# A decoder layer on one core: dense products issued whole or as four 32-column strips, score fills in 32x64 tiles

## The chip, the core and the metric

The kernel runs on one core of one Trainium2 chip. A core has five engines that run their own instruction streams and wait for each other at semaphores: TensorE (PE, matrix products; its weight loads are listed apart as PEld), VectorE (DVE), ScalarE (ACT), GpSimd (POOL) and SyncE (SP, which here issues DMA). Matrix products read SBUF and write PSUM, which has eight banks of 2 KB for each of 128 partitions.

TensorE's array has 128 rows (the contraction) and 128 columns (the outputs). It can be used whole, or divided into tiles that work side by side: 128 rows by 32 columns gives four tiles ("strips"), 32x128 gives four, 32x64 eight, 64x32 eight. The tile that a product uses follows from the partitions of its operands and of its output.

The metric is the device time of one execution in microseconds (us), the median of the runs.

## What is computed

One decoder layer over x of 16 batches x 512 tokens x 256 channels: a gated long convolution with an MLP, then causal self-attention and cross-attention with 16 heads of 16 channels, then a low-rank FFN, each with a residual and a layernorm.

```python
z = rmsnorm(u, pre_w) @ in_w.T                 # three projections, a 3-tap convolution, a long convolution
y = (yconv + xv * D_skip) * x2 ; y = y @ out_w.T + u
zm = rmsnorm(y, post_w)
x = layernorm(x + y + gelu(zm @ l1.T) * (zm @ l2.T) @ l3.T)      # l1, l2: 256 -> 672
...
q, k, v = heads(x @ Wq + bq), heads(x @ Wk + bk), heads(x @ Wv + bv)
y = softmax(mask(q k^T / 4)) v + softmax(qc kc^T / 4) vc         # 512 own keys, 64 cross keys
x = layernorm(x + y @ Wp + bp)
...
P = x @ U1 ; H = gelu(P @ V1 + b1) ; Q = H @ U2                  # 256 -> 64 -> 1024 -> 64 -> 256
x = layernorm(x + Q @ V2 + b2)
```

## The kernel before

Everything is float32, and each product then takes two passes through the array (two weight loads and two matmul records in the trace); a transposition takes one. The kernel has two stages. The first (to about 300 us) does the projections and the long convolution for all batches. The second goes through the 16 batches: `first_block` (gate, output projection, MLP), `attention` and `ffn`.

No engine's order is written by hand. Each piece of work is handed to `Plan.op` (line 78) with the engines that can run it, an estimated cost, a priority and the buffers that it holds; `Plan.schedule` (line 103) plays the program through with those costs, always takes the startable piece with the best rank, and `emit` issues the result. The instructions of every engine are thus in a fixed order, which overlaps three batches: batch b's attention runs beside the MLP of b+1 and the FFN of b-1. A piece on PE names its tiling; `change` (line 95) adds to its rank: staying in a divided shape is favoured by `STAY` (1000), and a piece that isn't urgent is held back by `HOLD` (1000) when it would leave the whole shape. `EMPTY` is the planner's allowance for a change of shape.

What runs on PE in the second stage, with the tile shape that each uses before:

- dense products, whole (128x128): `to_tokens` L1083, `outp` L1148, the MLP's L1187 and L1239, values L1268, context keys L1292 and values L1317, queries and keys L1340, the FFN's ends L1761 and L1807;
- transpositions, whole: L348, L1359, L1507;
- score fills, 32x128: `maxima` L1435 (12 per batch) and the exponentials' fills in `sums` L1557 (10 per batch), four heads side by side; the cross-attention's L1615 (2 per batch) in 32x64;
- weighted sums L1587 and the MLP's remainder L1217, strips (128x32); the cross sums L1635, 64x32;
- the FFN's middle: L1778 (64x128, two tiles) and L1794 (128x64, two tiles).

All score fills, of `maxima`, of `sums` and of the cross-attention, write one buffer: the pool `scores` has a single tile of four banks. A fill of `maxima` is read by DVE (a mask, L1484, and two or three maxima, L1486 to L1497); in batches 0, 1, 13, 14 and 15 ACT copies it out instead (L1458). A fill of `sums` or of the cross-attention is read by ACT's exponential (L1527). The next fill of any kind waits until that reader is done. In batches 0, 1 and 15 the fills are cut in two halves. The other products share three banks (`mm`) and one accumulator bank (`av`).

```python
"scores": tiles(psum, "scores", 1, [P, HPG, T]),
"av": tiles(psum, "av", 1, [P, T]),
"mm": tiles(psum, "mm", 3, [P, T]),
```

## Time and profile before

| | |
|---|---|
| time, median of 3 runs | 2083.39 us (2082.22 to 2087.12) |
| the profiled execution, its span | 2082.0 us |
| matmul records on PE | 14900 |
| granted TensorE clock, mean | 0.992 |
| DVE, ACT, POOL busy | 1331.5, 1029.1, 768.5 us |

The profile is of one execution. In its list of groups, a line is a line of the kernel, `out<-in` names the tiles, `128*32 128x512` is a matmul with 128 contraction rows and 32 output columns that streams 512 columns. Matmuls are pipelined: the length of one record holds the way through the array, so that what a product costs is read from start to start.

### The profile page before, as it was taken

The page shows a single profiled execution, that of the slowest core. Times are in us where ns is not written, and L with a number is a line of the kernel's source. Part 1 is how long each engine was busy: PE and PEld are TensorE (multiplying, and loading weights), DVE is VectorE, ACT ScalarE, POOL GpSimd, SP SyncE. Part 2 cuts the span into 40 slices and gives each one's busy share as a digit, 9 for nine tenths or more (in the row PEclk, how much of TensorE's full clock was granted, in tenths as well). Part 3 has the DMA queues.
Part 4 walks back from the last instruction along what each step waited for, and adds up shares of the span by engine and source line. Part 5 has one row for each costly group of instructions (what it writes and reads, how often), then busy time and mean ns, then how long its engine had stood idle before and what let it go on. Part 6 is the DMA issues. An engine that isn't in the chain of part 4 may idle for free. (4 is left out here: it accounts for less than half of the span.)

```text
span 2082.0 us, 36834 instructions
## 1 busy us (share of the span) xinstructions
PE 2005.5 (96%) x14900; PEld 1054.2 (51%) x14900; DVE 1331.5 (64%) x1922; ACT 1029.1 (49%) x1463; POOL 768.5 (37%) x1036
## 2 busy tenths in 40 slices
PE   8999978999999999999999999999999999999987
PEld 4455645555554545454545454454545454545443
DVE  7987543736584848484857576666767584656554
ACT  7863422656435262717161626253534446655773
POOL 7694622243323241414142424232323233533432
PEclk9999989999999999999999999999999999999999
DMA  5365861040304040313131312222131404031200
GB/s 200 109 211 179 269 221 51 6 119 17 119 11 144 12 134 22 123 33 118 37 108 48 100 56 88 68 71 85 58 98 33 123 13 129 17 101 44 72 22 31
DMA packets 114939, 182.22 MB, mean 88 GB/s; under 512 B 13393, under 2 KB 62034, under 8 KB 114642
## 3 DMA queue, kind: packets, MB, share of 16 engines
q1 hardware_dynamic: 113234, 177.26, 27.6%
q8 instruction: 117, 1.92, 0.4%
q10 hardware_dynamic: 1536, 2.62, 0.4%
q14 instruction: 52, 0.43, 0.1%
HBM read 111.09 MB, written 68.76 MB: 86 GB/s over the span
## 5 line engine op out<-in xcount | busy, mean ns | idle before, releaser
L1527 ACT ACTIVATE ex<-scores 128x2048 f32<-128x2048 f32 (+1 forms) x228 | 362.5, 1606 | 193.4 <-PE scores L1557 140.8
L1187 PE MATMUL mm<-xT,w_l 128*128 128x512 f32 x640 | 299.5, 608 | 0.0
L1574 POOL TENSOR_SCALAR_AFFINE_SELECT ex<-ex 128x512 f32<-128x512 f32 x256 | 159.1, 637 | 324.5 <-ACT ex L1527 323.1
L1435 PE MATMUL scores<-keys,q 32*128 32x192 f32 (+5 forms) x2848 | 225.3, 426 | 6.2 <-ACT ex L1458 4.6
L1557 PE MATMUL scores<-q,keys 32*128 32x256 f32 (+3 forms) x2240 | 183.3, 435 | 11.8 <-ACT ex L1527 10.9
L1435 PEld LDWEIGHTS scores<-keys,q 32*128 32x128 f32 x2848 | 123.8, 184 | 138.5 <-issue 41.1
L1786 ACT ACTIVATE row<-mm,b_s 128x512 f32<-128x512 f32 x124 | 79.0, 687 | 224.6 <-PE mm L1778 223.9
L1187 PEld LDWEIGHTS mm<-xT,w_l 128*128 128x128 f32 x640 | 114.5, 190 | 141.4 <-issue 133.9
L1717 POOL TENSOR_TENSOR nd<-nd,nd 128x1024 f32<-128x1024 f32 x30 | 70.8, 2358 | 299.2 <-DMA nd<-di 299.2
L1587 PE MATMUL av<-ex,va 128*32 128x512 f32 (+3 forms) x2048 | 164.8, 438 | 0.9 <-POOL ex L1574 0.9
L1239 PE MATMUL mm<-w_l,gT 128*128 128x256 f32 x640 | 160.6, 386 | 0.0
L308 POOL TENSOR_SCALAR small<-small 128x4 f32<-128x4 f32 (+1 forms) x66 | 13.3, 201 | 393.7 <-DVE small L1047 358.8
L500 DVE SCALAR_TENSOR_TENSOR frow<-fmm,cw,frow 128x511 f32<-128x511 f32 x192 | 141.1, 744 | 25.9 <-ACT frow L492 21.2
L1484 DVE TENSOR_TENSOR scores<-scores,mask_qk 128x1024 f32<-128x1024 f32 x132 | 115.6, 876 | 60.9 <-PE scores L1435 57.8
L1557 PEld LDWEIGHTS scores<-q,keys 32*128 32x128 f32 x2240 | 96.9, 184 | 107.5 <-ACT ex L1527 67.0
L1199 ACT ACTIVATE row<-mm 128x512 f32<-128x512 f32 x80 | 47.8, 598 | 209.4 <-PE mm L1187 209.4
L1458 ACT COPY ex<-scores 128x1024 f32<-128x1024 f32 (+1 forms) x96 | 114.4, 1228 | 65.6 <-PE scores L1435 52.9
L485 PE MATMUL fmm<-fx,inw 128*128 128x512 f32 x312 | 143.4, 604 | 0.0
L1239 PEld LDWEIGHTS mm<-w_l,gT 128*128 128x128 f32 x640 | 117.2, 190 | 44.6 <-issue 31.1
L299 DVE COPY row<-av 128x512 f32<-128x512 f32 x60 | 41.5, 692 | 134.9 <-PE av L1587 124.5
L1340 PE MATMUL mm<-xT,wqc_s 128*128 128x512 f32 x256 | 126.3, 611 | 0.0
L1346 DVE TENSOR_SCALAR q<-mm,bqc_s 128x512 f32<-128x512 f32 x62 | 46.5, 750 | 100.4 <-PE mm L1340 100.3
(212 smaller groups left out, 3489.3 us busy)
## 6 DMA issues: line engine op xcount, KB each, us to landing
dn<-row SPq DMA_DIRECT2D x120, 256.0 KB
keys<-dk SPq DMA_DIRECT2D x64, 256.0 KB
nd<-dn SPq DMA_DIRECT2D x30, 512.0 KB
nd<-di SPq DMA_DIRECT2D x30, 512.0 KB
fx<-hpad SPq DMA_DIRECT2D x28, 512.0 KB
early<-gates SPq DMA_DIRECT2D x16, 512.0 KB
early<-yconv SPq DMA_DIRECT2D x32, 256.0 KB
dk<-row SPq DMA_DIRECT2D x32, 256.0 KB
```

Of the source, the lines that this page charges most:

```text
L485: nc.tensor.matmul(ps.t, inw[:, k, bass.ts(m, P)], xT.t[:, k, :], start=(k == 0), stop=(k == KD - 1))
L500: lambda e, lag=lag: nc.vector.scalar_tensor_tensor(t.t[:, lag:], ps.t[:, 0 : T - lag], cw[:, m, 2 - lag : 3 - lag], t.t[:, lag:], ALU.mul ...
L1187: nc.tensor.matmul(ps.t, w[:, k, bass.ts(f, P)], zT.t[:, k, :], start=(k == 0), stop=(k == KD - 1))
L1239: nc.tensor.matmul(ps.t[:, bass.ts(cc, D)], gT.t[:, f, bass.ts(c, P)] if f < NF else gE.t, w_l3[:, f, :] if f < NF else w_l3e[:, c, :], st ...
L1340: nc.tensor.matmul(ps.t, w[:, k, cols], xT.t[:, k, :], start=(k == 0), stop=(k == KD - 1))
L1435: nc.tensor.matmul(sc.t[:, r, lo:hi], q.t[hd, bass.ts(i, P)], kk.t[hd, k0 - at + lo : k0 - at + hi], start=True, stop=True,)
L1458: lambda e, sc=sc, both=both, cols=cols: nc.scalar.copy(both.t[:, :, cols], sc.t[:, :, cols]),
L1484: nc.vector.tensor_tensor(diag, diag, mask, ALU.add)
L1527: lambda e: nc.scalar.activation(ex.t.rearrange("p (r n) -> p r n", r=HPG)[:, :, cols], sc.t[:, :, cols], AF.Exp, scale=scale),
L1557: nc.tensor.matmul(sc.t[:, r, lo:hi], keys[g].t[hd, TC + j * P : TC + (j + 1) * P], qas[g].t[hd, q0 + lo : q0 + hi], start=True, stop=True,)
L1574: lambda e, ex=ex, at=at: nc.gpsimd.affine_select(out=ex.t.rearrange("p (r n) -> p r n", r=HPG)[:, :, at : at + P], in_=ex.t.rearrange("p ...
L1587: nc.tensor.matmul(av[g].t[bass.ts(r, SLOT), j * P :], va.t[:, j, h * VS : h * VS + SLOT], ex.t[:, r * T + at : r * T + at + n], start=(j ...
```

## The change

Products whose shape fits both get `flex=True`: the planner issues them whole when the array is whole, and otherwise as four products of 32 output columns each (`Plan.matmul`), so that they can follow the weighted sums, or one another, without a change of shape. Whole and strips are now both "plain" shapes, in which staying isn't favoured. All score fills use 32x64 (two products of 64 columns for each head), the FFN's L1778 uses 64x32 and its L1794 strips. The planner's allowances for a change of shape get other values, and are looked up by the shape entered instead of the one left. As the planner's costs and ranks change, the order on every engine changes too; the amount of work on DVE, ACT, POOL and SP is the same but for ten copies that go to DVE instead of ACT.

```diff
+STRIPS = (P, SLOT)
...
-    EMPTY = {P: 0.215, P // 2: 0.16, P // 4: 0.145}
+    EMPTY = {P: 0.2, P // 2: 0.148, P // 4: 0.121}
...
     def change(self, o, tiling):
-        if o.tiling == tiling:
-            return -self.STAY if tiling != FULL else 0
+        want, plain = self.mode(o, tiling), (FULL, STRIPS) if self.strips else (FULL,)
+        if want == tiling:
+            return -self.STAY if tiling not in plain else 0
         if o.urgent or o.tiling == FULL:
             return 0
-        return self.HOLD if tiling == FULL else -self.STAY / 2
+        return self.HOLD if tiling in plain else -self.STAY / 2
+
+    def mode(self, o, tiling):
+        return (tiling if tiling in (FULL, STRIPS) else STRIPS) if o.flex else o.tiling
+
+    def matmul(self, out, weights, moving, **kw):
+        rows, cols = self.now
+        n = weights.shape[-1]
+        for c in range(0, n, cols):
+            cs = slice(c, min(c + cols, n))
+            self.nc.tensor.matmul(out[cs], weights[:, cs], moving, **kw)
...
-                    o.empty = self.EMPTY[tiling[1]]
-                    tiling = o.tiling
+                    o.used = self.mode(o, tiling)
+                    if o.used != tiling:
+                        o.empty = self.EMPTY[o.used[1]]
+                    tiling = o.used
...
-    ROWS4, ROWS2, COLS4, COLS2, BOTH = (SLOT, P), (P // 2, P), (P, SLOT), (P, P // 2), (P // 2, SLOT)
+    COLS2, ROWS, BOTH = (P, P // 2), (SLOT, P // 2), (P // 2, SLOT)
...
-    plan = Plan(pool, 1000, 1000)
+    plan = Plan(pool, 1000, 1000, nc)
...
-                    gelus_pe[b].append(plan.op("PE", pe(T), mm, p1 - k, r=[(zT, k)], w=[ps]))
+                    gelus_pe[b].append(plan.op("PE", pe(T), mm, p1 - k, r=[(zT, k)], w=[ps], flex=True))
...
-                        "PE", cost_pe / len(cuts), mm, ps_, r=[q, kk], w=[(sc, h)], tiling=ROWS4, urgent=True
+                        "PE", cost_pe / len(cuts), mm, ps_, r=[q, kk], w=[(sc, h)], tiling=ROWS, urgent=True
...
             def hm(e, fp=fp, bank=bank):
-                for s in range(2):
-                    half = bass.ts(s, RANK)
-                    nc.tensor.matmul(bank(s), v1_s[half, bass.ts(fp, P)], pT.t[half, :], start=True, stop=True)
+                for c in range(0, P, SLOT):
+                    for s in range(2):
+                        half, at = bass.ts(s, RANK), fp * P + c
+                        plan.matmul(bank(s)[c : c + SLOT], v1_s[half, at : at + SLOT], pT.t[half, :], start=True, stop=True)
-            gelus_pe[window].append(plan.op("PE", tiled(T), hm, p3, r=[pT], w=hp, tiling=ROWS2))
+            gelus_pe[window].append(plan.op("PE", tiled(T), hm, p3, r=[pT], w=hp, tiling=BOTH))
...
-            plan.op("PE", tiled(T), qm, p3 - 1, r=hT, w=[acc], tiling=COLS2)
+            plan.op("PE", tiled(T), qm, p3 - 1, r=hT, w=[acc], tiling=STRIPS)
```

The other dense products get `plan.matmul` and `flex=True` in the same way. The first stage's plan is made without `nc`, so nothing in it is issued in strips; its order moves a little with the allowances.

More of the change, by code (lines that the diff above doesn't have):

```diff
@@ L58, in __init__ @@
         self.ready, self.start, self.end, self.engine = 0.0, None, None, None
-        self.tiling, self.urgent = FULL, False
+        self.tiling, self.urgent, self.flex, self.used = FULL, False, False, FULL
 class Plan:
@@ L70, with __init__, op @@
     CROSS = 0.18
-    def __init__(self, tiles, hold=0, stay=0):
+    def __init__(self, tiles, hold=0, stay=0, nc=None):
         self.tiles, self.ops = tiles, []
         self.HOLD, self.STAY = hold, stay
-    EMPTY = {P: 0.215, P // 2: 0.16, P // 4: 0.145}
-    def op(self, engines, cost, fn, prio, r=(), w=(), lat=0.0, after=(), tiling=FULL, urgent=False, holds=()):
+        self.nc, self.strips, self.now = nc, nc is not None, FULL
+    EMPTY = {P: 0.2, P // 2: 0.148, P // 4: 0.121}
+    def op(
+        self, engines, cost, fn, prio, r=(), w=(), lat=0.0, after=(), tiling=FULL, urgent=False, holds=(), flex=False
+    ):
         o = Op(len(self.ops), engines.split(), cost, lat, prio, fn)
-        o.tiling, o.urgent = tiling, urgent
+        o.tiling, o.urgent, o.flex = tiling, urgent, flex
         self.ops.append(o)
@@ L162, in schedule @@
                 o.engine, o.start = e, now
-                if e == "PE" and o.tiling != tiling:
-                    o.empty = self.EMPTY[tiling[1]]
-                    tiling = o.tiling
-                else:
-                    o.empty = 0.0
+                o.empty = 0.0
+                if e == "PE":
+                    o.used = self.mode(o, tiling)
+                    if o.used != tiling:
+                        o.empty = self.EMPTY[o.used[1]]
+                    tiling = o.used
                 until[e] = now + o.empty + (o.cost[o.engines.index(e)] if isinstance(o.cost, tuple) else o.cost)
@@ L193, in emit @@
                 b.t = self.tiles[b.cls][b.slot[1]]
+            self.now = o.used
             o.fn(o.engine)
@@ L698, in near_mm @@
                         )
-            plan.op("PE", 1.0, near_mm, pc - 60, r=[XV[kh], NEAR], w=[ps], tiling=COLS4, holds=[st])
+            plan.op("PE", 1.0, near_mm, pc - 60, r=[XV[kh], NEAR], w=[ps], tiling=STRIPS, holds=[st])
             def evac_state(e, ps=ps, st=st, blk=blk):
@@ L760, in far_mm @@
                             )
-            far_done = plan.op("PE", 1.0, far_mm, pc + 10, r=[st, far], w=ys, tiling=(SLOT, P // 2))
+            far_done = plan.op("PE", 1.0, far_mm, pc + 10, r=[st, far], w=ys, tiling=ROWS)
             for c in range(HPG):
@@ L1082, in mm @@
                     def mm(e, cp=cp, cc=cc, k=k, ps=ps):
-                        nc.tensor.matmul(
+                        plan.matmul(
                             ps.t[:, bass.ts(cc, D)], xT.t[:, k, bass.ts(2 * cp + cc, P)], w[:, k, :],
@@ L1086, in mm @@
                         )
-                    plan.op("PE", pe(D), mm, prio, r=[xT], w=[ps])
+                    plan.op("PE", pe(D), mm, prio, r=[xT], w=[ps], flex=True)
             add_op(ps, res, res, cp, prio)
@@ L1147, in outp @@
                     def outp(e, cp=cp, cc=cc, k=k, ps=ps):
-                        nc.tensor.matmul(
+                        plan.matmul(
                             ps.t[:, bass.ts(cc, D)], yt.t[:, k, bass.ts(2 * cp + cc, P)], outw[:, k, :],
@@ L1151, in outp @@
                         )
-                    plan.op("PE", pe(D), outp, p0, r=[(yt, k)], w=[ps], after=after)
+                    plan.op("PE", pe(D), outp, p0, r=[(yt, k)], w=[ps], after=after, flex=True)
             add_op(ps, x_, y1, cp, p0)
@@ L1186, in mm @@
                     def mm(e, f=f, w=w, k=k, ps=ps):
-                        nc.tensor.matmul(
+                        plan.matmul(
                             ps.t, w[:, k, bass.ts(f, P)], zT.t[:, k, :], start=(k == 0), stop=(k == KD - 1)
                         )
-                    gelus_pe[b].append(plan.op("PE", pe(T), mm, p1 - k, r=[(zT, k)], w=[ps]))
+                    gelus_pe[b].append(plan.op("PE", pe(T), mm, p1 - k, r=[(zT, k)], w=[ps], flex=True))
                     if f == HOLD:
@@ L1216, in mm_e @@
                     for c in range(NT):
-                        nc.tensor.matmul(
+                        plan.matmul(
                             ps.t[bass.ts(c, FE), bass.ts(n, P)], w[:, k, NF * P :], zT.t[:, k, bass.ts(c, P)],
@@ L1220, in mm_e @@
                         )
-        gelus_pe[b].append(plan.op("PE", 0.88, mm_e, p1, r=[zT], w=[ps], tiling=COLS4))
+        gelus_pe[b].append(plan.op("PE", 0.88, mm_e, p1, r=[zT], w=[ps], tiling=STRIPS))
         gelus[b].append(plan.op(
@@ L1238, in mm @@
                     def mm(e, c=2 * cp + cc, cc=cc, f=f, ps=ps):
-                        nc.tensor.matmul(
+                        plan.matmul(
                             ps.t[:, bass.ts(cc, D)],
@@ L1244, in mm @@
                         )
-                    plan.op("PE", pe(D), mm, p2, r=[(gT, f) if f < NF else gE], w=[ps])
+                    plan.op("PE", pe(D), mm, p2, r=[(gT, f) if f < NF else gE], w=[ps], flex=True)
             add_op(ps, x_, x_, cp, p2)
@@ L1267, in mm @@
                     def mm(e, jp=jp, jj=jj, k=k, ps=ps):
-                        nc.tensor.matmul(
+                        plan.matmul(
                             ps.t[:, bass.ts(jj, D)], xT.t[:, k, bass.ts(2 * jp + jj, P)], wv_s[:, k, :],
@@ L1271, in mm @@
                         )
-                    plan.op("PE", pe(D), mm, p0 + 40, r=[(xT, k)], w=[ps])
+                    plan.op("PE", pe(D), mm, p0 + 40, r=[(xT, k)], w=[ps], flex=True)
             plan.op(
@@ L1291, in kc_mm @@
                 for g in range(G):
-                    nc.tensor.matmul(
+                    plan.matmul(
                         ps.t[:, bass.ts(g, 2 * TC)], wck_s[:, bass.ts(g, P)], ctxT[:, b * TC : (b + 2) * TC],
@@ L1295, in kc_mm @@
                     )
-            plan.op("PE", 0.9, kc_mm, p0, w=[ps], after=begun)
+            plan.op("PE", 0.9, kc_mm, p0, w=[ps], after=begun, flex=True)
             plan.op(
@@ L1316, in attention @@
             "PE", pe(D),
-            lambda e, ps=ps: nc.tensor.matmul(
+            lambda e, ps=ps: plan.matmul(
                 ps.t[:, 0:D], twice.t.rearrange("c s t -> c (s t)"), wcv_s, start=True, stop=True
             ),
-            p0 + 45, r=[twice], w=[ps],
+            p0 + 45, r=[twice], w=[ps], flex=True,
         )
@@ L1339, in mm @@
                 def mm(e, k=k):
-                    nc.tensor.matmul(ps.t, w[:, k, cols], xT.t[:, k, :], start=(k == 0), stop=(k == KD - 1))
-                plan.op("PE", pe(T), mm, prio - k, r=[(xT, k)], w=[ps], holds=[dst])
+                    plan.matmul(ps.t, w[:, k, cols], xT.t[:, k, :], start=(k == 0), stop=(k == KD - 1))
+                plan.op("PE", pe(T), mm, prio - k, r=[(xT, k)], w=[ps], holds=[dst], flex=True)
             def ev(e):
@@ L1434, in mm @@
                                 hd = bass.ts(r, SLOT)
-                                nc.tensor.matmul(
+                                plan.matmul(
                                     sc.t[:, r, lo:hi], q.t[hd, bass.ts(i, P)], kk.t[hd, k0 - at + lo : k0 - at + hi],
@@ L1556, in mm @@
                                 hd, q0 = bass.ts(r, SLOT), j * P - at
-                                nc.tensor.matmul(
+                                plan.matmul(
                                     sc.t[:, r, lo:hi], keys[g].t[hd, TC + j * P : TC + (j + 1) * P],
@@ L1564, in sums @@
                         "PE", sum(tiled((T - j * P) // len(parts)) for _, j in uses), mm, p1 + 13,
-                        r=[x for kq in kqs.values() for x in kq], w=[(sc, h)], tiling=ROWS4, urgent=True,
+                        r=[x for kq in kqs.values() for x in kq], w=[(sc, h)], tiling=ROWS, urgent=True,
                     ))
@@ L1586, in wm @@
                             h = g * HPG + r
-                            nc.tensor.matmul(
+                            plan.matmul(
                                 av[g].t[bass.ts(r, SLOT), j * P :], va.t[:, j, h * VS : h * VS + SLOT],
@@ L1598, in sums @@
                         cost, wm, weights = wms.pop((g, j))
-                        plan.op("PE", cost, wm, pb_ - 6, r=[va, *weights], w=[av[g]], tiling=COLS4)
+                        plan.op("PE", cost, wm, pb_ - 6, r=[va, *weights], w=[av[g]], tiling=STRIPS)
                         left[g] = left[g][1:]
@@ L1614, in cm @@
                         for n in range(2):
-                            nc.tensor.matmul(
+                            plan.matmul(
                                 sc.t[bass.ts(n, TC), r, cols], kcs.t[hd, b % 2, g + n, :], cqas[g + n].t[hd, cols],
@@ L1621, in cross_scores @@
                     "PE", tiled(T // len(parts)) + 0.05, cm, p1 + 13, r=[kcs, cqas[g], cqas[g + 1]], w=[(sc, h)],
-                    tiling=(SLOT, P // 2), urgent=True,
+                    tiling=ROWS, urgent=True,
                 ))
@@ L1634, in cwm @@
                         part = bass.ts(half, TC)
-                        nc.tensor.matmul(
+                        plan.matmul(
                             cavs[half].t[bass.ts(r, SLOT), :], vc.t[part, g * HPG // 2 + r, :],
@@ L1760, in pt @@
             def pt(e, k=k, ps=ps):
-                nc.tensor.matmul(ps.t, u1_s[:, k, :], x2T.t[:, k, :], start=(k == 0), stop=(k == KD - 1))
-            plan.op("PE", pe(T), pt, p3 - k, r=[(x2T, k)], w=[ps])
+                plan.matmul(ps.t, u1_s[:, k, :], x2T.t[:, k, :], start=(k == 0), stop=(k == KD - 1))
+            plan.op("PE", pe(T), pt, p3 - k, r=[(x2T, k)], w=[ps], flex=True)
         plan.op("ACT DVE", (act(T), dve(T)), lambda e, ps=ps: copy(e, pT.t, ps.t), p3, r=[ps], w=[pT])
@@ L1793, in qm @@
                 for s in range(2):
-                    nc.tensor.matmul(
+                    plan.matmul(
                         acc.t[bass.ts(s, RANK), :], u2_s[:, 2 * fp + s, :], hT[s].t,
@@ L1806, in om @@
                 for cc in range(2):
-                    nc.tensor.matmul(
+                    plan.matmul(
                         ps.t[:, bass.ts(cc, D)], qT.t[:, bass.ts(2 * cp + cc, P)], v2_s, start=True, stop=True
                     )
-            plan.op("PE", 2 * pe(D), om, p4, r=[qT], w=[ps])
+            plan.op("PE", 2 * pe(D), om, p4, r=[qT], w=[ps], flex=True)
             add_op(ps, x_, x_, cp, p4)
```

## The prediction

> **What bounds the kernel now.** The page first: who is busy, and where in the span.

> ```profile
> span 2082.0 us, 36834 instructions
> PE 2005.5 (96%) x14900; PEld 1054.2 (51%) x14900; DVE 1331.5 (64%) x1922; ACT 1029.1 (49%) x1463; POOL 768.5 (37%) x1036
> ...
> PE   8999978999999999999999999999999999999987
> ```

> Then the same in a stretch of the steady batches, and PE's waits from 500 to 1700 us:

> ```profile
> 800.00:900.00 100.00, 99.67 (x712) 50.65 (x709) 64.86 (x93) 46.40 (x60) 31.76 (x44) 1.00 0.24 76
> ```
> ```profile
> PE scores L1557 <- ACT ex L1527: 3.0, 9, 0.3
> PE scores L1435 <- DVE maxes L1495: 1.1, 1, 1.1
> PE mm L348 <- ACT row L1786: 0.2, 1, 0.2
> ```

> PE is busy 99.67 of 100 us at full clock, and waits 4.3 us in 1200. So PE sets the time: what is taken from PE counts in full, and so does every wait that PE gets in exchange. The last view is the order of time around two changes of shape and around one fill of the maxima:

> ```profile
> 1199.55 1.50 PE L1587 MATMUL av<-ex,va 128*32 128x512 f32 x16
> 1200.98 1.13 PE L1268 MATMUL mm<-wv_s,xT 128*128 128x256 f32 x4
> 1202.04 1.11 PE L1615 MATMUL scores<-q,kcs 32*64 32x512 f32 x16
> 1203.08 1.08 PE L1217 MATMUL mm<-xT,w_l 128*32 128x128 f32 x32
> 1203.32 1.88 ACT L1527 ACTIVATE ex<-scores 128x2048 f32<-128x2048 f32 x1 [1.67 <-PE scores L1615]
> ...
> 1207.31 1.15 PE L1435 MATMUL scores<-keys,q 32*128 32x320 f32 x16
> 1208.53 1.23 DVE L1484 TENSOR_TENSOR scores<-scores,mask_qk 128x1024 f32<-128x1024 f32 x1 [0.49 <-PE scores L1435]
> 1209.80 0.69 DVE L1486 TENSOR_REDUCE maxes<-scores 128x8 f32<-128x512 f32 x1
> 1210.40 1.22 DVE L1489 TENSOR_REDUCE maxes<-scores 128x4 f32<-128x1024 f32 x1
> 1211.54 0.68 DVE L1492 TENSOR_REDUCE maxes<-scores 128x4 f32<-128x512 f32 x1
> ```

> How it is read: inside one shape, the trace's matmul starts follow each other by 0.429 us (512 columns), 0.216 (256) and 0.109 (128), however many tiles work side by side. The four passes of L1268 should take 0.863, but from its start to the next line's start is 1.06: 0.197 is the change of shape. It has two parts, the first weight load, which nothing covers (0.104 for 128 columns, 0.051 for 64, 0.024 for 32), and the emptying of the shape left (0.09 to 0.14). The fill L1435 has streamed its last column at 1208.28, DVE starts 0.25 later and is done at 1212.22, 3.69 after its start. The fill L1615, with eight tiles, has streamed at 1202.95 and ACT starts 0.37 later.

> **The change part by part.**

> **Strips instead of whole products: 0.** The order of the built programs has 28,218 matmuls instead of 14,900, but the passes, counted as groups that run side by side, are the same in both, and sum to 1756 us. The row L1217 shows strips at the pace of whole products: 32 matmuls of 128 columns are eight groups at 0.109, the four of a group starting within 0.02. The cover of the added instructions is the pass itself; without it, four starts of 0.0066 each would add 0.02 a pass.

> [...]

> **Changes of shape: -44.4 us.** Counted in the two orders, priced by the median of the same change in the trace. Before, 1082: into whole 386 x 0.213, into 32x128 353 x 0.198, strips 141 x 0.139, 128x64 80 x 0.153, 64x128 50 x 0.207, 32x64 40 x 0.145, 64x32 32 x 0.133: 204.4 us. After, 977: into strips 389 x 0.157, into 32x64 388 x 0.158, whole 103 x 0.222, 64x32 80 x 0.153, 128x64 17 x 0.15: 160.0 us. The count falls by a tenth only, since each score fill still stands between dense products; it is the entry that gets cheaper. Of the new prices, 32x64 to strips (313 times) is measured, 0.158 in 24 cases. Strips to 32x64 (297 times) stands in the trace only with a wait in it: I take 0.163, whole to 32x64 (0.143, 29 cases) and 0.020 for the later start of the last strip (the same difference as 0.217 to 0.197 into 32x128). Its bounds are 0.138 and 0.217, the least into 64 columns and strips into 128: -7 to +16 us. In one pair of steady batches PE's work falls from 213.7 to 208.4 us, 2.6 a batch.

> **What the new order then waits for: +40 us in ten steady batches.** All fills go through one buffer, so between two fills PE needs other work for as long as the reader takes. After the 320+192 fill that is 0.37 + 3.69 + 0.05 (DVE's end to PE's start, in the trace) = 4.1 us. Batch by batch, the order before has 4.5 to 5.1 us there. The order after has 4.8, 5.5 and 4.6 after the first three, but after the fourth only three dense products of 256 columns: 3 x 0.432 and two changes of shape, 1.62 us. PE then waits 2.5 us. Behind that fill stands everything on PE, next the FFN's middle; its second bank is freed by a residual addition (L1094) that comes behind the same maxima in DVE's queue: 0.7. Three more short places (transpositions for the FFN behind ACT's gelu and norms, the 512 fill with 3.27 against 3.45, the FFN's first product behind ACT's copy) give 0.8. That is 4.0 in a batch; the wait of 1.05 that the FFN's middle has before (L1778's second tile starts 1.0 late for its bank) is there in both. Batches 2 to 11 have this order: 10 x 4.0. The exponentials' fills keep 2.47 or more, against 0.37 + 1.94 + 0.05 = 2.36: no wait. Bounds: 25 (the fill alone) and 48 (0.8 more, should the second FFN pair wait twice).

> **The last batches: +18.5 us.** In batch 14 the last three fills of the maxima and the first of the exponentials follow with nothing between; before there are 2.57 us each time. Each waits for a whole reader, 2.36, and the one ahead of them has 1.18: 8.5 us in four waits. In the last batch PE's work between the last maxima is 1.18, 1.18 and 2.05 and ends with transpositions that need the last of them; dense work was used up earlier. I take 10, from four readers of 2.4 to 3.7 less what stands there; bounds 0 (the work comes back behind it) and 16 (as much again as the idle time that PE has after 1900 us now).

> **Eight tiles reach the reader later: +7 us.** 0.37 against 0.25 for each fill. In the steady batches the other work covers it. In batches 0, 1 and 15 fill follows reader at once: some 60 fills x 0.12. Bounds 0 and 14 (every half fill of five batches).

> [...]

> **The sum**: 2082.0 - 44.4 + 40 + 18.5 + 7 = 2103 in the profiled execution; the median of the runs lies 1.4 above it: 2104 us.

> **The rivals.**

> *The changes cost less in the new shapes.* Place: strips to 32x64, 297 times. At 0.10 instead of 0.163 the sum is back at 2085, from 0.08 on it is a gain: 2079. [...] Against it: strips to every other shape show 0.137 or more with a 0.113 emptying. Chance 0.10.

> *It cancels.* The first wait of a batch alone (25), batch 14 (8.5) and nothing in the last: 2082 - 44 + 34 + 7 + 1 = 2080, up to 2089 with half of the last batch. For it: DVE is 64% busy, so order alone makes these waits. Against it: the fill, the reader and the next fill are in a fixed order. Chance 0.14.

> *The longer instruction stream costs too.* The first stage has PE waits put down to issue, 8.6 us from 177 to 265 us, where small matmuls come densest. With 1.9 times the matmuls the same in the second stage gives another 9 to 18: 2113 to 2122. Against it: the steady batches show no such wait. Chance 0.12.

> *The waits don't come*, as the order would have PE late enough: 2040. PE would have to be 2.5 us behind DVE there; nothing shows it. Chance 0.03.

> **How the numbers follow.** The forecast, slower with its own range 2092 to 2113, has 0.61; with the third rival, slower has 0.73. Faster: most of the first rival and the last, and a part of the second, 0.13. Within 0.3%, 2077 to 2090 (about what a measurement of this kernel can tell from no change): 0.14. The range reaches down through the second rival and up to the third: 2077 to 2122.

> **What would show it.** PE's records: 28,218. DVE's last maximum of a 320+192 fill (L1511 after) should be what PE's score fills wait for: ten times 2.5 us. The stretch 800 to 900 should show PE at 96 to 97 of 100, not 99.7, and the last slices of the span less than now. Strips: dense rows with 128*32 at 0.43 from start to start. A fill's reader should start 0.37 after the last column. Wrong if PE stays above 99 in the steady batches, or if a change of shape into 32x64 from strips measures under 0.12.

## The result and the profile after

The changed kernel takes 2110.43 us, the median of four runs (2106.35 to 2114.77), against 2083.86 for the kernel before beside it (2082.22 to 2087.12): a ratio of 1.0126, 95% interval 1.0107 to 1.0145. The profiled execution spans 2107.5 us, 25.5 more than that of before.

The page of the changed kernel, with the same rows that were read of before and the row of the granted clock:

```profile
span 2107.5 us, 63441 instructions
...
PE 1979.1 (94%) x28218; PEld 865.7 (41%) x28218; DVE 1334.5 (63%) x1931; ACT 1023.0 (49%) x1454; POOL 769.9 (37%) x1036
...
PE   8999878999999999999999999999999999989787
...
PEclk9999989999999999999999999999999999999999
```

PE is busy for 26 us less and the span is 26 us longer: what was saved on PE came back twice over as idle time. By these rows nine instructions moved from ACT to DVE, where ten copies were named ahead. The steady stretch that showed 99.67 of 100 before (the columns are PE, PEld, DVE, ACT, POOL, then the granted clock, DMA share and GB/s):

```profile
800.00:900.00 100.00, 97.27 (x1488) 38.81 (x1490) 65.65 (x95) 45.09 (x58) 33.34 (x44) 1.00 0.26 77
```

PE's waits between 500 and 1700 us in the changed kernel (us in all, times, the longest):

```profile
PE scores L118 <- DVE maxes L1511: 21.8, 9, 2.4
PE mm L118 <- ACT xT L320: 2.4, 10, 0.2
PE mm L367 <- ACT row L1806: 2.2, 9, 0.2
PE scores L118 <- ACT ex L1546: 1.4, 3, 0.7
```

The first row is the wait that the forecast named: nine in this stretch and a tenth after it, each of 2.42 us. One of them in order of time, with the work of PE and DVE around it:

```profile
1037.90 2.34 PE L118 MATMUL mm<-wp_s,xT 128*32 128x256 f32 x40
...
1040.17 1.12 PE L118 MATMUL scores<-keys,q 32*64 32x320 f32 x32
...
1041.22 1.50 PE L118 MATMUL mm<-wp_s,xT 128*32 128x256 f32 x24
1041.40 1.23 DVE L1503 TENSOR_TENSOR scores<-scores,mask_qk 128x1024 f32<-128x1024 f32 x1 [0.37 <-PE scores L118]
1042.66 0.69 DVE L1505 TENSOR_REDUCE maxes<-scores 128x8 f32<-128x512 f32 x1
1043.27 1.22 DVE L1508 TENSOR_REDUCE maxes<-scores 128x4 f32<-128x1024 f32 x1
1044.40 0.68 DVE L1511 TENSOR_REDUCE maxes<-scores 128x4 f32<-128x512 f32 x1
...
1045.14 1.13 PE L118 MATMUL scores<-keys,q 32*64 32x448 f32 x32 [2.42 <-DVE maxes L1511]
```

The fill's last pass starts at 1040.92 and streams 192 columns in 0.16, so its last column is through at 1041.08, and DVE starts 0.31 later (the 0.37 in the brackets is how long DVE had been idle, another thing). DVE works from 1041.40 to 1045.08, and PE starts 0.06 later. PE has three products of `wp_s` to put in between (24 matmuls, six groups of four), as the built order said. The same view shows the pace of strips: from 1037.90 to 1040.17 stand ten groups of 0.216 and 0.11 for the emptying of the strips. The other part of the change of shape, 0.05 for the first weight load, shows behind the fill's first pass.

Where the 25.5 us come from can be added up from the starts of all matmul records. Each step from one group of side-by-side matmuls to the next is split into the streaming of its columns, the median price of its change of shape, what the stretches at half clock cost (the profile's granted clock is 0.5 there), and the rest, which is waiting (us). The streaming is counted at the pace of each width and is the same in both by construction, so a slower pace would show as waiting:

| profiled execution | streaming | changes of shape | half clock | waiting | span |
|---|---|---|---|---|---|
| before | 1755.3 | 202.0 | 13.0 | 95.0 | 2082.0 |
| changed kernel | 1755.3 | 156.0 | 23.0 | 156.7 | 2107.5 |
| difference | 0 | -46.0 | +10.0 | +61.7 | +25.5 |

About 17 us before the first and after the last matmul make up each span. By place (cut at the same piece of work in both traces), the changed kernel is 0.5 us late at 768 us, 5.6 late at 1533 us after seven more batches, and 25.5 late at the end: the last 555 us, with the batches whose fills are copied or cut, lose 20.

### The profile page after: what moved, and what is told of

It is laid out like the page before. It is cut to its first block, busy times and chain, and to the rows that moved or that the text cites. A ratio compares the mean times of both kernels' runs of the same rounds, so it can differ in the third digit from the quotient of the medians.

```text
span 2107.5 us, 63441 instructions
## 1 busy us (share of the span) xinstructions
PE 1979.1 (94%) x28218; PEld 865.7 (41%) x28218; DVE 1334.5 (63%) x1931; ACT 1023.0 (49%) x1454; POOL 769.9 (37%) x1036
## 5 line engine op out<-in xcount | busy, mean ns | idle before, releaser
L118 PE MATMUL mm<-xT,w_l 128*32 128x512 f32 (+2 forms) x2946 | 311.6, 541 | 0.0
L1593 POOL TENSOR_SCALAR_AFFINE_SELECT ex<-ex 128x512 f32<-128x512 f32 x256 | 159.3, 637 | 293.3 <-ACT ex L1546 292.1
L118 PE MATMUL scores<-keys,q 32*64 32x192 f32 (+5 forms) x5696 | 222.0, 413 | 37.4 <-DVE maxes L1511 24.2
L1806 ACT ACTIVATE row<-mm,b_s 128x512 f32<-128x512 f32 x124 | 78.7, 685 | 308.0 <-PE mm L118 303.8
L118 PE MATMUL scores<-q,keys 32*64 32x256 f32 (+3 forms) x4480 | 180.7, 422 | 11.8 <-ACT ex L1546 9.2
L118 PEld LDWEIGHTS scores<-keys,q 32*64 32x64 f32 x5696 | 104.2, 133 | 189.0 <-DVE maxes L1511 37.4
L1503 DVE TENSOR_TENSOR scores<-scores,mask_qk 128x1024 f32<-128x1024 f32 x132 | 115.6, 876 | 83.4 <-PE scores L118 83.4
L118 PEld LDWEIGHTS mm<-xT,w_l 128*32 128x32 f32 (+1 forms) x2946 | 90.8, 111 | 181.4 <-issue 167.8
L118 PE MATMUL mm<-w_l,gT 128*32 128x256 f32 (+1 forms) x2332 | 159.5, 383 | 0.0
L519 DVE SCALAR_TENSOR_TENSOR frow<-fmm,cw,frow 128x511 f32<-128x511 f32 x192 | 140.9, 744 | 25.5 <-ACT frow L511 20.9
L327 POOL TENSOR_SCALAR small<-small 128x4 f32<-128x4 f32 (+1 forms) x66 | 13.3, 202 | 372.3 <-DVE small L1066 337.2
L118 PEld LDWEIGHTS scores<-q,keys 32*64 32x64 f32 x4480 | 79.7, 131 | 121.0 <-ACT ex L1546 70.2
L118 PE MATMUL mm<-xT,wqc_s 128*32 128x512 f32 (+1 forms) x874 | 125.9, 596 | 0.3 <-DVE q L1535 0.3
L118 PEld LDWEIGHTS mm<-w_l,gT 128*32 128x32 f32 (+1 forms) x2332 | 82.7, 113 | 81.9 <-issue 43.8
L511 ACT ACTIVATE frow<-fmm,cb,cw 128x512 f32<-128x512 f32 x96 | 74.0, 776 | 70.8 <-PE fmm L504 55.9
```

The costliest lines, as they stand in the source:

```text
L118: self.nc.tensor.matmul(out[cs], weights[:, cs], moving, **kw)
L511: lambda e: nc.scalar.activation(t.t, ps.t, AF.Identity, bias=cb[:, m : m + 1], scale=cw[:, m, 2:3]),
L519: lambda e, lag=lag: nc.vector.scalar_tensor_tensor(t.t[:, lag:], ps.t[:, 0 : T - lag], cw[:, m, 2 - lag : 3 - lag], t.t[:, lag:], ALU.mul ...
L1503: nc.vector.tensor_tensor(diag, diag, mask, ALU.add)
L1593: lambda e, ex=ex, at=at: nc.gpsimd.affine_select(out=ex.t.rearrange("p (r n) -> p r n", r=HPG)[:, :, at : at + P], in_=ex.t.rearrange("p ...
L1806: lambda e, f=f, s=s, bank=bank, dst=hT[s]: nc.scalar.activation(dst.t, bank(s), AF.Gelu_apprx_tanh, bias=b1_s[:, f : f + 1]),
```

## Experiments

The new kernel differs from the old in the shapes and, because the planner is told of them, in the order of work on every engine. The first six kernels part the two: they fix one order and issue it in other shapes. In all of them the order of DVE, ACT, POOL and SP is exactly that of the kernel named, and PE's too but for the strips.

**The order of before, all shapes of the change.** `schedule` plans with the old tilings and allowances (`old=`); `emit` then picks each product's shape along PE's order.

```diff
     def emit(self):
+        tiling = FULL
...
+            if o.engine == "PE":
+                tiling = o.used = self.mode(o, tiling)
             self.now = o.used
...
-                        "PE", cost_pe / len(cuts), mm, ps_, r=[q, kk], w=[(sc, h)], tiling=ROWS, urgent=True
+                        "PE", cost_pe / len(cuts), mm, ps_, r=[q, kk], w=[(sc, h)], tiling=ROWS, old=(SLOT, P), urgent=True
```

> Every engine's order is that of the kernel before (the planner sees the old shapes and allowances); products are issued in the shapes of the change (strips beside strips, fills in 32x64, the FFN's middle in 64x32 and strips). Counted in this order: 992 changes of shape, 162.5 us by the prices of the forecast, against 1082 and 204.4. Theory (the shapes pay as priced, the loss is the new order's waits): 2083 - 42 + 7 (eight-tile fills reach their reader later in batches 0, 1, 15) + up to 8 for readers that the faster PE now waits for = 2048 to 2056. Rival (strips and eight-tile fills cost as much as they save, the order is innocent): 2080 to 2110.

Measured: 2047.24 us (median of 4), ratio to before 0.9824 (0.981 to 0.9838): faster than both kernels. Its page, the steady stretch and PE's waits from 500 to 1700 us:

```profile
span 2044.6 us, 63257 instructions
...
PE 1961.6 (96%) x28074; PEld 866.6 (42%) x28074; DVE 1328.0 (65%) x1922; ACT 1029.9 (50%) x1463; POOL 769.9 (38%) x1036
```
```profile
800.00:900.00 100.00, 99.56 (x1448) 40.12 (x1451) 67.38 (x98) 46.18 (x59) 31.82 (x44) 1.00 0.27 82
```
```profile
PE scores L117 <- ACT ex L1547: 4.6, 14, 0.4
PE scores L117 <- DVE maxes L1515: 1.3, 1, 1.3
PE mm L368 <- ACT row L1807: 0.2, 1, 0.2
```

With 28,074 matmul records, nearly the changed kernel's number, PE is back at 99.56 of 100, and of the waits for the last maximum a single one of 1.3 us is left. By the same sum, the changes of shape take 159.3 us, waiting 100.5, half clock 12.7. The time is 0.8 below the stated range: waiting rose by 5.5, where 7 to 15 had been expected. The shapes pay as priced; the rival is out.

**The order of the changed kernel, the shapes of before.** The planner sees the new shapes, `emit` issues the old ones.

```diff
-            self.now = o.used
+            self.now = o.old
```

> Every engine's order is that of the changed kernel; dense products are whole, fills 32x128 and the FFN's middle as before. Counted: 1146 changes of shape, 215.3 us (+11). Theory (the order makes the waits): +11, ten steady batches at 2.3 + 0.8 us = +31, the last two batches +20, the clock after long waits +8: 2083 + 70 = 2153, 2135 to 2165. Rival (the order is innocent): 2083 + 11 = 2094, 2085 to 2102.

Measured: 2160.16 us (median of 5), 1.0369 (1.0353 to 1.0384). Its waits between 500 and 1700 us have the same rows on top:

```profile
PE scores L118 <- DVE maxes L1511: 20.9, 9, 2.3
PE mm L118 <- ACT xT L320: 2.1, 9, 0.2
PE mm L367 <- ACT row L1805: 1.7, 9, 0.2
```

Changes 212.9, half clock 22.0, waiting 150.9: against before +10.9, +9.0 and +55.9. The long wait belongs to the order and comes with either set of shapes.

**Single shapes in the order of before.** Fills alone, then strips alone, then both (the FFN's middle left in its old shapes). One line of each, against the kernel before:

```diff
-                        "PE", cost_pe / len(cuts), mm, ps_, r=[q, kk], w=[(sc, h)], tiling=ROWS4, urgent=True
+                        "PE", cost_pe / len(cuts), mm, ps_, r=[q, kk], w=[(sc, h)], tiling=ROWS, old=(SLOT, P), urgent=True
```
```diff
-                    plan.op("PE", pe(D), mm, prio, r=[xT], w=[ps])
+                    plan.op("PE", pe(D), mm, prio, r=[xT], w=[ps], flex=True)
```

> The kernel before in its own order, with the score fills alone in 32x64. Counted: 1082 changes, 192.8 us (-11.6). Theory: -11.6 and +7 for the later reader in batches 0, 1, 15: 2079, 2074 to 2086. Rival (the later reader counts at every fill, 384 x 0.12 = 46): 2117. PE's waits in the steady batches stay below 3 us a batch by the theory.

> The kernel before in its own order, dense products as strips where strips stand before them, fills in 32x128. 3531 more matmul instructions. Counted: 1019 changes, 179.5 us (-24.9). Theory: 2083 - 25 = 2058, 2055 to 2064. Rival (each added instruction costs: a fetch or an issue of 4 ns or more each, +14 or more): 2070 or more.

> The order of the kernel before, fills in 32x64 and dense products as strips beside strips, the FFN's middle in its old shapes. Counted: 1019 changes of shape, 167.6 us (-36.8). Theory (prices add up as counted, the two parts measured alone gave -8 and -23): 2083.5 - 36.8 + 4 = 2051, 2047 to 2056, so that the FFN's middle is worth the remaining 3 to 5 us. Rival (the parts help only together with the FFN's shapes): 2053 or more by -8 and -23 alone, with no gain from strips standing before 64-column fills.

| in the order of before | counted, us | measured, us | ratio (95%) |
|---|---|---|---|
| fills in 32x64 | -11.6 | 2075.95 | 0.9956 (0.9942 to 0.9969) |
| dense strips | -24.9 | 2061.05 | 0.9889 (0.9875 to 0.9904) |
| both | -36.8 | 2050.43 | 0.9851 (0.9836 to 0.9866) |
| both and the FFN's middle | -41.9 | 2047.24 | 0.9824 (0.981 to 0.9838) |

The first three lie within their stated ranges, and fills alone leave PE's waits in the steady batches below 2 us of 100 by the same sum, as they were before. The three steps measure -8, -23 and -33 us. The last 3 us, for the FFN's middle, are no larger than these intervals can tell. That the parts add up is the theory's point; here the rival's bound (2053 or more) was too close to be cleanly told from it.

**Strips everywhere.** The order of before again, with dense products as strips even beside whole transpositions.

```diff
+                tiling = o.used = STRIPS if o.flex else o.tiling
```

> The order of the kernel before, all three shapes of the change, but dense products are always strips, beside whole transpositions too: 15,186 matmuls in the program instead of 14,445, 1053 changes of shape, 171.0 us (+8.5 against the run with the order before). Theory (a strip costs nothing, a change of shape what it cost elsewhere): 2047 + 8.5 = 2056, 2052 to 2060. Rival (staying whole after a transposition brings nothing, since leaving it costs the same): 2047.

Measured: 2051.06 us (median of 4), 0.9845 (0.9831 to 0.9859), 3.8 above the run with the order before and one below the stated range. Its changes of shape take 167.5 us, 8.2 more, as counted; its waiting is 2.9 less. PE has 29,556 records, twice those of before, and is busy 99.83 of 100 us between 800 and 900: more instructions cost nothing that can be seen. The 8.2 speak against the rival, by which leaving the two shapes costs the same; the time alone, 3.8 more, lies between the rival and the theory.

```profile
800.00:900.00 100.00, 99.83 (x1525) 38.46 (x1528) 67.27 (x98) 46.34 (x60) 32.19 (x44) 1.00 0.27 82
```

**Why the order is short of work there.** The change also gave the planner lower allowances for a change of shape: 0.121 into strips and 0.148 into 64 columns, where the trace has 0.157 and 0.158. This kernel edits that one line:

```diff
-    EMPTY = {P: 0.2, P // 2: 0.148, P // 4: 0.121}
+    EMPTY = {P: 0.222, P // 2: 0.158, P // 4: 0.157}
```

> The changed kernel with one line edited: the planner's allowances for a change of shape are the medians that the trace of the changed kernel shows (whole 0.222, 64 columns 0.158, strips 0.157) instead of 0.2, 0.148, 0.121. Counted in its order: PE's stream and changes 1915.1 us (the run with the order before and the new shapes: 1918.3), and between 500 and 1600 us PE's work falls short of fill and reader by 6 us in all (28 us after the 320+192 and 512 fills in the changed kernel: not there). Theory (the allowances were too low, so the plan put PE ahead of DVE, and its order has too little work behind the fourth 320+192 fill): 2047 - 3 = 2044, 2038 to 2052, no wait of 2.4 us behind the last maximum, no half clock in the steady batches. Rival (dense work as strips is taken early whatever the allowance): 2085 to 2110.

Measured: 2077.37 us (median of 7), 0.9972 (0.9961 to 0.9982). The theory is half right: the named wait is gone and with it the half clock in the steady batches (13.3 us in all, as before), but the time is 33 us above what was expected. Its waits from 500 to 1700 us, and the place in order of time:

```profile
PE mm L118 <- ACT row L1806: 12.8, 21, 0.9
PE scores L118 <- ACT ex L1546: 7.2, 13, 1.1
PE mm L118 <- ACT xT L320: 2.4, 10, 0.2
PE scores L118 <- DVE maxes L1511: 0.7, 1, 0.7
```
```profile
1033.53 1.12 PE L118 MATMUL scores<-keys,q 32*64 32x320 f32 x32
...
1036.55 1.07 PE L118 MATMUL mm<-wp_s,xT 128*32 128x256 f32 x16 [0.31 <-ACT row L1806]
...
1039.27 1.12 PE L118 MATMUL scores<-keys,q 32*64 32x448 f32 x32
1040.32 1.09 PE L118 MATMUL mm<-row,v_s 64*32 64x512 f32 x16
1042.30 1.66 PE L118 MATMUL mm<-row,v_s 64*32 64x512 f32 x16 [0.89 <-ACT row L1806]
```

The 448+64 fill now starts without a wait. But the count looked only at fills and their readers. In this order the FFN's products wait for banks that ACT's gelu (L1806) empties, 1.6 us a batch, and one wait of 6.4 us, behind DVE's L1535, stands in the last batch. Against the run with the order of before and the same shapes, waiting is 34.4 us more (134.9 against 100.5), changes of shape 3.7 less. These two make up some two thirds of it; the rest was not taken apart.

**An allowance above every price.** The same line, with 0.2 for all three shapes.

```diff
+    EMPTY = {P: 0.2, P // 2: 0.2, P // 4: 0.2}
```

> The changed kernel with one line edited: the allowance is 0.2 for every shape, above the measured 0.157 and 0.158. Counted in its order: stream and changes 1912.7 us, short by 5.5 us between 500 and 1600 us. Theory: 2047 - 6 = 2041, 2036 to 2050. Rival (only the right prices give a good order): above 2060.

Measured: 2082.51 us (median of 11), 0.9996 (0.9985 to 1.0007): the expectation missed by 41 us. The steady batches are good, if not quite as hoped (between 768 and 1527 us of before it gains 16.6 us, the order of before with the same shapes about 19), but by 671 us it is 14 us behind, and waits 42.7 us in the last stretch, against 26.8 in the order of before. More than half of the 14 arises in the second of the 16 batches, whose fills ACT copies out:

```profile
494.11 1.31 PE L118 MATMUL scores<-keys,q 32*64 32x256 f32 x48 [1.51 <-ACT ex L1477]
497.44 2.01 PE L118 MATMUL scores<-keys,q 32*64 32x256 f32 x48 [2.02 <-ACT ex L1477]
501.58 2.02 PE L118 MATMUL scores<-keys,q 32*64 32x256 f32 x32 [2.13 <-ACT ex L1477]
505.68 2.01 PE L118 MATMUL scores<-q,keys 32*64 32x256 f32 x32 [2.08 <-ACT ex L1477]
509.78 2.02 PE L118 MATMUL scores<-q,keys 32*64 32x256 f32 x48 [2.09 <-ACT ex L1546]
```

Four fills with nothing between them follow the first one, and the five wait 9.8 us; the granted clock from 500 to 510 us is 0.50. The count, from 500 to 1600 us and 5.5 us in all, does not hold them. So neither the right prices nor generous ones give a good order by themselves. That the low allowances made the short place behind the fourth 320+192 fill is shown only this far: in the orders built with the change's three allowances scaled by 1.1, 1.2 and 1.4, with 0.2 flat, with the old values and with the measured ones it is not there; scaled by 0.8 to 1.05 it is, and by 0.7 another fill of the maxima is short by as much.

**The fewest changes of shape, an order known to be bad.** The measured allowances, and the planner's delay between engines raised.

```diff
-    CROSS = 0.18
+    CROSS = 0.30
```

> The measured allowances, and the planner's delay from one engine to the next 0.30 instead of 0.18. Counted in its order: stream and changes 1910.6 us, the least of all, but between 500 and 1600 us PE's work behind a fill falls short of the reader by 132 us (90 fills of the exponentials with 1.3 us where 2.36 are needed: 95; cross fills 12; maxima 26), against 6. Theory (what a kernel takes is the count of stream, changes and short places, whatever the planner believed): 2047 - 8 + 126 + 12 in the last batches = 2177; 2120 if half is met by other waits; to 2190. Rival (the fewest changes of shape win): 2040.

Measured: 2194.27 us (median of 4), 1.0538 (1.0523 to 1.0552), 4 above the stated range. Its waits:

```profile
PE scores L118 <- ACT ex L1546: 89.5, 91, 1.5
PE av L118 <- ACT row L1806: 7.1, 14, 0.8
PE scores L118 <- DVE maxes L1511: 4.3, 6, 2.5
```

The 90 short fills of the exponentials counted in the built order are there, 91 waits of nearly 1 us, and the least streaming and changes of shape go with the longest time.

## Why the prediction was right

It said 2104 us, from 2077 to 2122, and slower at 0.73; 2110.43 was measured. By its steps:

*Strips at no cost: right.* Strips of 256 columns follow each other at 0.216 and of 512 at 0.429, as whole products do, and with strips everywhere waiting does not grow (2.9 us less than in the order of before with the change's shapes, at 29,556 records instead of 28,074).

*Changes of shape, -44.4: right, -46.0.* The one price that had to be taken from its neighbours, strips to 32x64 at 0.163, measures 0.164 (median of 297). With it the first rival falls: it needed 0.10.

*Waits in ten steady batches, +40 with bounds of 25 and 48: right in kind and place, too large in size.* The 2.5 us behind the fourth 320+192 fill came ten times, 24.9 in all from start to start. Of the other 1.5 a batch, the two waits behind ACT are there (0.41 for the transpositions behind the gelu, 0.40 for the FFN's first product behind ACT's copy). The 0.7 for the FFN's second bank, freed by a residual addition behind the maxima, failed: the wait there is 0.99 a batch, as it was before (1.10). And the wait of 0.40 that before had ahead of a fill of the exponentials went away, which the step left out. All waits of one batch are 4.3 us, against 1.5 before: +2.8 instead of +4.0.

*The last batches, +18.5: the reasons given are there, the size was too small.* Batch 14's fills, back to back:

```profile
1886.33 1.12 PE L118 MATMUL scores<-keys,q 32*64 32x320 f32 x32 [1.02 <-ACT ex L1477]
1889.52 1.65 PE L118 MATMUL scores<-keys,q 32*64 32x448 f32 x32 [2.06 <-ACT ex L1477]
1893.13 2.02 PE L118 MATMUL scores<-keys,q 32*64 32x512 f32 x16 [1.97 <-ACT ex L1477]
1897.17 2.02 PE L118 MATMUL scores<-q,keys 32*64 32x512 f32 x16 [2.02 <-ACT ex L1477]
```

These are the four waits, 1.1 and three of 2.3 from start to start: 7.9, and one of 1.0 behind them, against 8.5 forecast (its own terms, three of 2.36 and one of 1.18, add up to 8.3). In the last batch PE waits at the transpositions that need the last maxima:

```profile
1995.38 0.55 PE L1526 MATMUL mm<-ident,maxes 128*128 128x128 f32 x3 [1.97 <-DVE xt L1113]
1998.52 0.48 PE L1526 MATMUL mm<-ident,maxes 128*128 128x128 f32 x1 [2.59 <-DVE maxes L1516]
2002.20 3.63 PE L118 MATMUL mm<-row,v_s 64*32 64x512 f32 x18 [3.21 <-DVE q L1535]
```

From 1527 us (before) and 1533 (after) to the end, waiting grows by 29.1, half clock by 6.8, and the changes of shape fall by 15.7. Two of the ten steady batches' long waits lie in this stretch (5.6 at 2.8 a batch), so that some 23.5 are left where 18.5 and a part of the next term were forecast.

*Eight tiles reach the reader later, +7: right in kind, the price of one almost twice too large.* The forecast set DVE's start after a four-tile fill (0.25) against ACT's after an eight-tile one (0.37). The same reader shows half of that: DVE starts 0.25 after the last column of a four-tile fill (L1484, median of 88) and 0.31 after an eight-tile one (L1503, median of 106), 0.066 more. ACT starts at one of two times, 0.25 or 0.31 after four tiles and 0.31 or 0.37 after eight, again 0.06 apart. The forecast's 60 fills at 0.066 are 4 us, and fills alone add 4.4 us of waiting.

*What was missing: half clock, +10.0.* The forecast had no term for it, though the profile of before shows it up to 340 us (a granted clock of 0.69 from 330 to 340). It is what the waits above cost a second time: the five stretches at half clock between 900 and 2010 us each begin behind 3.413 us in which PE was idle for 0.58 to 0.71 of the time.

*The sum is nearer than its terms, and that part is luck.* Waits were forecast at 65.5 and measured 61.7, but the ten steady batches took 28 instead of 40, the last ones some 23.5 instead of 18.5, and some 10 stand ahead of the steady batches, where the forecast had only a part of the 7. With the half clock's 10.0 on top, 2103 for the execution became 2107.5. Not luck are the prices of the changes of shape and the place, the cause and the length of the longest wait.

The other rivals: it did not cancel; the instruction stream cost nothing that can be seen (the profile's queue q8, instruction, has 221 packets instead of 117, but the table of waits lists no wait for issue from 500 to 1700 us, and the 9.9 us that it lists for the whole execution, against 8.7 before, stand in the first stage, where nothing is issued in strips by the change); the waits came.

## What to carry to other kernels

Where engines follow a fixed order, judge a change of instruction shapes in two parts, by issuing the new shapes in the old order: here that was worth -36.6 us, and the new order that came along lost all of it and 27 more. Of the five orders that were timed with the new shapes, the one of before is the fastest, by 30 us. Count in the built order the work that stands between a buffer's reader and its next writer, from measured durations, and do so for every buffer, the FFN's banks as well as the score buffer, and from the first batch to the last; a total of work or of shape changes alone picks the wrong order. When one program beats its neighbours only by its order, keep that order rather than plan it anew.

## What the runs showed of the hardware

```profile
920.00:930.00 10.00, 10.00 (x197) 5.03 (x185) 9.54 (x14) 0.00 (x0) 0.00 (x0) 1.00 0.01 3
930.00:940.00 10.00, 7.56 (x121) 2.53 (x105) 9.04 (x14) 1.75 (x3) 1.64 (x4) 0.83 0.00 0
940.00:950.00 10.00, 9.75 (x113) 3.65 (x114) 7.68 (x15) 7.63 (x10) 4.08 (x4) 1.00 0.01 2
```

Each cost about 1.5 us more in the steady batches (4.4 for three).

Eight side-by-side tiles instead of four moved the reader's start by more than the tiles' own spacing: DVE started 0.25 us after the last column of a fill with four tiles (L1484 of before) and 0.31 after one with eight (L1503 of the changed kernel), while tiles start 0.0066 apart, which makes 0.026 for four more.
